# Selective scan in a two-layer vision kernel: tiles of four states by 32 channels instead of two states by 64

## The chip, the cores and the metric

The kernel runs on one core of one Trainium2 chip. The metric is the device time of one execution in microseconds (us). Before the change it was 23158.47 us, the median of three runs (23155.23 to 23162.02).

## The reference

Two residual layers act on `x` of shape (8, 64, 64, 192); each is fed the group-normed input. Layer 0 is a Mamba-2 block with convolutions and an MLP; the change leaves its work alone. Layer 1 is a four-direction selective scan (SS2D), per image of 4096 pixels:

```python
xz = einsum('bhwc,dc->bhwd', x, in_proj_w); xc, z = split(xz)          # 384 channels each
xc = silu(depthwise_conv3x3(xc) + conv_b)
xs = [xc by rows, xc by columns, and both reversed]                     # K = 4 sweeps
dts, B, C = split(einsum('bkdl,kcd->bkcl', xs, x_proj_weight))          # 12 + 16 + 16 rows
delta = softplus(einsum('bkrl,kdr->bkdl', dts, dt_projs_weight) + bias)
A = -exp(A_logs)                                                        # (4, 384, 16 states)
# for every pixel, in order:
h = exp(delta * A) * h + (delta * u) * B                                # per channel and state
y = sum over states of h * C
out = (layernorm(sum of the four sweeps' y + xs * Ds) * silu(z)) @ out_proj_w.T
```

So every sweep of every image runs 384 x 16 recurrences over 4096 pixels, in float32.

## The kernel before, in words

Layer 1 works image by image (8 images). For each image a planner (`Flow`) interleaves three things in one stretch: `finish` of the image before (layer norm, gate, output projection), `front` of this one (projection, 3x3 convolution, copies of the result in DRAM: `xo[0]` by rows, `xo[1]` by columns, `xo[2]` by tokens) and the `prologue` of its scan. The planner orders each engine's instructions by weights written beside each step. Then `main()` runs the scan, whose instructions stay in the order in which the code issues them, engine by engine.

The scan of an image has 32 *steps*: 4 sweeps of 8 chunks of 512 pixels (`TT`). A step has 24 *units*: here 8 pairs of states `p` (in the order of `ORDER`) by 3 channel blocks `d` of 128 channels. I number the units of a step q = 0 to 23. A tile of a unit has 128 partitions, two states by 64 channels, and two halves `f` of 512 pixels, for two groups of 64 channels. One turn of the loop in `main()` for unit u issues, in this order:

- `load_c` (at d = 0): C rows of a later pair, repeated over 64 partitions, into `cb` (3 buffers).
- `run(u)`: two scan instructions on VectorE (DVE), one per half: `hs` from the decays `ea`, the inputs `g` in PSUM and the carried state `cy` (L1662); then on GpSimd (POOL) the copy of the last column into `cy` (L1674) and the multiplication by `cb` (L1676).
- `decay(u + 2)`: two exponentials on ScalarE (ACT) into `ea` (L1620), which has 3 buffers: the tile of unit u + 2 is that of unit u - 1.
- two or three `weigh`: ACT multiplies the turned product delta*u of one 128-pixel block by one state's B (L1605), into `pw` (8 buffers). Of 16 states x 4 blocks a step weighs 56; the list `todo` runs 2 instructions past what the next pair needs (10 are made ahead, a pair needs 8 or 6).
- `supply(u + 1)`: TensorE (PE) transposes the blocks of `pw` into `g` (L1646), 4 buffers of one half. For 4 of 32 pair-blocks (`on_diagonal`) it multiplies delta*u by a diagonal matrix of B instead (`dg`, L1634), with no `weigh`.
- `collect(u - 2)`: PE sums over the two states with `sel`, one matmul of 64 output partitions per half, side by side (L1691); in sweep 0 the skip term is added there (L1689). `add(u - 3)`: DVE adds a finished `y` to `yacc`.
- pieces of `prepare(s + 1)`, the next step's inputs, placed at fixed q: loads (q 0), `project` (2 to 4), `keep` (5: `xdbl`), `turn_b` and `keep_b` (6, 7), then for three blocks `step` (PE, `p_dt`), `soft` (ACT exp and ln, `spa`; at q 8, 10, 13), `delta` (DVE, `de`), `turn` and `keep_du` (`duT`), and `repeat_delta`, which copies delta over the partitions (`dr`).

A float32 matmul stands in the profile as two MATMUL records, a transpose as one. All DMAs are issued by SP in one queue, which waits in order.

Of the kernel before, what the change touches and what calls it, by code (L numbers as in the profile page):

```python
# [16 lines left out]
CP, CT = 96, 2  # L17
# [12 lines left out]
NP1 = N // 2  # L30
ND = 8
ORDER = [0, 4, 1, 5, 2, 6, 3, 7]
# [1001 lines left out]
def layer1(tc, consts, x1s, mv1, out, w_in, w_x, w_dt, w_out):  # L1034
# [7 lines left out]
    with ExitStack() as ctx:  # L1042
# [9 lines left out]
        wi = wp.tile([CP, CT, 2 * DIN], F32, name="wi1")  # L1052
# [7 lines left out]
        an = wp.tile([128, K, NP1, 2 * DT], F32, name="an")  # L1060
# [6 lines left out]
        sel = wp.tile([128, 64], F32, name="sel")  # L1067
        for i in range(2):
            nc.vector.tensor_copy(sel[i * 64 : i * 64 + 64], ident[i * 64 : i * 64 + 64, i * 64 : i * 64 + 64])
# [24 lines left out]
        zero = yacc[:, 0, : ND * 128].rearrange("p (n b) -> p n b", b=128)  # L1094
        nc.gpsimd.memset(zero, 0.0)
        dzs = [dgp.tile([ND, 128 * 128], F32, name=f"dz{i}") for i in range(2)]
        for t in dzs:
            nc.sync.dma_start(out=t.rearrange("n (a b) -> a n b", b=128), in_=zero)

        def scaled(w, b, half):  # L1100

            for ct in range(CT):
                r = yield step(
                    "ACT",
                    0.6,
                    lambda: [
                        nc.scalar.activation(
                            w[:, ct],
                            wi[:, ct, half * DIN : half * DIN + DIN],
                            AF.Copy,  # L1110
                            scale=sc[:, b * CT + ct : b * CT + ct + 1],
                        )
                    ],
                )
            return r
# [326 lines left out]
        def scan(xo):  # L1442
# [11 lines left out]
            units = [(s, p, d) for s in range(len(steps)) for p in ORDER for d in range(DT)]  # L1454
# [3 lines left out]
            def first(s):  # L1458
                return steps[s][1] == (0 if steps[s][0] < 2 else NS1 - 1)

            def prepare(s, bank=lambda name: mp.tile([128, TT], F32, name=name, tag="mm")):
# [5 lines left out]
                def load():  # L1467
                    st["xc"] = pools["pr1"].tile([128, DT, TT], F32, name="xc")
                    o(nc.sync.dma_start(out=st["xc"], in_=xo[k % 2][:, :, c * TT : c * TT + TT]))
                    st["ut"] = pools["pr1"].tile([128, NB1, DIN], F32, name="ut", bufs=1)  # L1470
                    if k % 2 == 0:
                        src = xo[2][c * TT : c * TT + TT].rearrange("(j p) m -> p j m", p=128)
                        o(nc.sync.dma_start(out=st["ut"], in_=src))
                    else:
                        for i in range(2):
                            src = xo[2].rearrange("(h w) m -> w h m", w=WI)[c * RT + i : c * RT + RT : 2]
                            o(nc.sync.dma_start(out=st["ut"][i * 64 : i * 64 + 64], in_=src.rearrange("j h m -> h j m")))
# [21 lines left out]
                def spread():  # L1499
                    dz = dzs[s % 2]  # L1500
                    st["dg"] = dg = pools["dg1"].tile([128, ND, 128], F32, name="dg")
                    o(nc.sync.dma_start(out=dz[:, :: 128 + 1], in_=xds[s % 2][N - ND : N, 0:128]))
                    o(nc.sync.dma_start(out=dg, in_=dz.rearrange("n (a b) -> a n b", b=128)))
# [11 lines left out]
                def keep_b():  # L1515
                    st["bt"] = bt = pools["pr1"].tile([128, NB1, N], F32, name="bt")
                    o(nc.vector.tensor_copy(bt.rearrange("p a b -> p (a b)"), st["p_b"][:, : NB1 * N]))
                    st["duT"] = pools["pr1"].tile([128, NB1, DIN], F32, name="duT")
# [31 lines left out]
                def keep_du(d):  # L1550
# [4 lines left out]
                            st["ut"][:, :, d * 128 : d * 128 + 128],  # L1555
# [12 lines left out]
                    9: [(delta, 0), (step, 1)],  # L1568
                    10: [(soft, 1)],
                    11: [(delta, 1), (turn, 0), (repeat_delta, s, 0)],  # L1570
                    12: [(keep_du, 0), (step, 2)],
                    13: [(soft, 2)],
                    14: [(delta, 2), (turn, 1)],
                    15: [(keep_du, 1)],
                    16: [(turn, 2)],
                    17: [(keep_du, 2)],
                    20: [(repeat_delta, s, 1)],
                    21: [(repeat_delta, s, 2)],
                }

            def repeat_delta(s, d):

                state[s]["dr", d] = dr = pools["dr1"].tile([128, 2, TT], F32, name="dr")
                de = state[s]["de", d]
                for f in range(2):
                    for i in range(2):
                        o(nc.sync.dma_start(out=dr[i * 64 : i * 64 + 64, f], in_=de[f * 64 : f * 64 + 64]))

            def load_c(s, p):
                state[s]["cb", p] = cb = pools["bc1"].tile([128, TT], F32, name="cb")  # L1590
                for i in range(2):
                    o(
                        nc.sync.dma_start(
                            out=cb[i * 64 : i * 64 + 64], in_=state[s]["cd"][2 * p + i].partition_broadcast(64)
                        )
                    )

            def weigh(s, p, j, i):

                st = state[s]  # L1600
                if i == 0:
                    st["pw", p, j] = pools["pw1"].tile([128, 2 * DT, 2, 64], F32, name="pw")
                n = 2 * p + i
# [3 lines left out]
                        st["duT"][:, j].rearrange("p (g c) -> p g c", c=64),  # L1607
# [5 lines left out]
            def decay(u):  # L1613
                s, p, d = units[u]
                k, c = steps[s]
                made["e", u] = ea = pools["e1"].tile([128, 2, TT], F32, name="ea")
                for f in range(2):
                    at = 2 * d + f
                    o(
                        nc.scalar.activation(  # L1620
                            ea[:, f], state[s]["dr", d][:, f], AF.Exp, scale=an[:, k, p, at : at + 1]
# [3 lines left out]
            def supply(u):  # L1625
                s, p, d = units[u]
                gs = [pools["g1"].tile([128, TT], F32, name="g") for f in range(2)]
                made["g", u, 0], made["g", u, 1] = gs
                for j in range(NB1):
                    if on_diagonal(p, j):  # L1630
# [302 lines left out]
```

## Time and profile before

| what | value |
|---|---|
| median of three runs | 23158.47 us |
| the profiled execution's own time | 23175.73 us |
| its span, first to last instruction | 23174.0 us |
| busy: PE, DVE, ACT, POOL | 94%, 91%, 87%, 70% |
| granted TensorE clock | 0.971 of full speed |
| DMA, one queue | 1976 MB, 31.9% of 16 engines |
| first scan instruction of image 1, its last | 7302.3 us, 9333.4 us: 2031.1 us for 32 steps |
| from there to the first scan of image 2 | 252.4 us |

"Busy" is the share of the span in which an engine had at least one instruction in flight; matmul ends are modelled, so a busy PE can have room left. Waits name what came last before an engine went on. Layer 0 takes the first fifth of the span; the eight scans follow, with a shorter stretch of front and finish between them.

### The profile page before, as it was taken

The numbers are of one execution on the slowest core, as the hardware profiler recorded it, in microseconds if no ns is written. First come the engines' busy times: TensorE is split into PE (matmuls) and PEld (weight loads), VectorE is DVE, ScalarE is ACT, GpSimd is POOL, SyncE is SP. The second block draws the span as 40 slices with busy tenths as digits, with TensorE's granted clock in tenths as the row PEclk, the third lists the DMA queues.
The fourth block names the chain that finished last, engine by engine and source line by source line (L and its number), as shares of the span: only waits on it lengthen the run. The fifth ranks groups of instructions, "written<-read, shape, count | busy, mean of one in ns | idle before, by whom it ended". The sixth has DMA issues, their size and how long they took to land.

```text
span 23174.0 us, 348545 instructions
## 1 busy us (share of the span) xinstructions
PE 21762.7 (94%) x118788; PEld 11070.5 (48%) x118788; DVE 21110.3 (91%) x22093; ACT 20048.9 (87%) x35418; POOL 16109.5 (70%) x12872
## 2 busy tenths in 40 slices
PE   8999999979998999899999999999999999999999
PEld 4444444435554555455545544554455445544554
DVE  7888888869998999899989998999899989998998
ACT  5666666759997999799979997999899989988998
POOL 1111111139995999599959995999599869976997
PEclk8999999989999999999999999999999999999999
DMA  1111111133333333333333334333433343333332
GB/s 52 45 44 41 45 45 45 42 96 92 95 93 111 92 92 94 111 94 93 90 114 93 92 87 117 95 92 88 117 92 92 89 117 93 93 91 113 92 94 75
DMA packets 1738653, 1998.38 MB, mean 86 GB/s; under 512 B 537280, under 2 KB 1034848, under 8 KB 1727648
## 3 DMA queue, kind: packets, MB, share of 16 engines
q1 hardware_dynamic: 1736864, 1976.07, 31.9%
q8 instruction: 934, 15.30, 0.3%
q14 instruction: 855, 7.00, 0.1%
HBM read 1360.20 MB, written 212.60 MB: 68 GB/s over the span
## 4 chain that ended last, share of the span: by engine, by line
PE 48%; ACT 22%; DVE 11%; POOL 8%; issue 6%; DMA 3%; SPq 2%; DVEq 0%; POOLq 0%; ACTq 0%
PE g L1646 10%; PE y L1691 10%; ACT ea L1620 10%; ACT pw L1605 9%; POOL hs L1676 7%; DVE hs L1662 3%; PE g L1634 3%; PE p_f L957 3%; DVE xs L1209 3%; PE p_d L1488 2%; PE p_x L450 2%; PE p_f L977 2%; PE p_dt L1523 2%; DMA dr<-de 2%; PE p_o L874 2%
## 5 line engine op out<-in xcount | busy, mean ns | idle before, releaser
L1676 POOL TENSOR_TENSOR hs<-hs,cb 128x1024 f32<-128x1024 f32 x6144 | 14584.3, 2374 | 496.4 <-POOL cy L1674 4.2
L1662 DVE TENSOR_TENSOR_SCAN hs<-ea,cy,g 128x512 f32<-128x512 f32 x10752 | 12894.9, 1258 | 187.2 <-PE g L1646 178.1
L1620 ACT ACTIVATE ea<-dr,an 128x512 f32<-128x512 f32 x12288 | 8139.8, 710 | 528.5 <-DVE hs L1662 507.0
L1605 ACT ACTIVATE pw<-duT,bt 128x384 f32<-128x384 f32 x14336 | 7832.7, 600 | 23.5 <-DVE duT L1552 23.5
L1691 PE MATMUL y<-hs,sel 128*64 128x512 f32 x24576 | 6635.2, 618 | 360.0 <-POOL hs L1676 338.6
L1646 PE MATMUL g<-ident,pw 128*128 128x128 f32 x43008 | 6089.9, 281 | 41.1 <-ACT pw L1605 4.8
L1646 PEld LDWEIGHTS g<-ident,pw 128*128 128x128 f32 x43008 | 4612.5, 141 | 2522.6 <-issue 1254.9
L1674 POOL COPY cy<-hs 128x2 f32<-128x2 f32 x6144 | 1160.7, 189 | 2262.0 <-DVE hs L1662 2228.8
L1634 PEld LDWEIGHTS g<-dg,duT 128*64 128x64 f32 x24576 | 1557.4, 136 | 2053.0 <-issue 1484.6
L1634 PE MATMUL g<-dg,duT 128*64 128x128 f32 x24576 | 2257.9, 282 | 169.4 <-DVE hs L1662 106.1
L1691 PEld LDWEIGHTS y<-hs,sel 128*64 128x64 f32 x24576 | 1234.2, 135 | 1563.0 <-issue 865.6
L1662 DVE TENSOR_TENSOR_SCAN hs<-ea,g 128x512 f32<-128x512 f32 x1536 | 1751.8, 1197 | 129.1 <-PE g L1646 116.8
L367 POOL TENSOR_TENSOR s<-xs 96x512 f32<-96x512 f32 x64 | 121.7, 1902 | 2139.6 <-DVE xs L345 1850.2
L1523 PE MATMUL p_dt<-xdbl,wd 13*128 13x512 f32 x1536 | 857.5, 639 | 96.2 <-DVE duT L1552 71.0
L1209 DVE SCALAR_TENSOR_TENSOR xs<-pad,p,xs 128x4096 f32<-128x4096 f32 x192 | 860.9, 4484 | 50.7 <-ACT xs L1199 43.5
L367 POOL TENSOR_TENSOR s<-sq 96x512 f32<-96x512 f32 x128 | 180.1, 1407 | 942.7 <-ACT sq L380 864.4
L1488 PE MATMUL p_d<-xc,wx 128*44 128x512 f32 x1536 | 788.6, 596 | 19.9 <-DMA xc<-xo 19.9
L957 PE MATMUL p_f<-h,wf 96*128 96x512 f32 x1536 | 762.4, 635 | 44.1 <-ACT zs L552 27.5
L345 DVE SCALAR_TENSOR_TENSOR x<-xx,p,x 96x512 f32<-96x512 f32 x1024 | 784.8, 816 | 15.2 <-ACT x L334 15.0
L345 DVE SCALAR_TENSOR_TENSOR xs<-xin,p,xs 96x512 f32<-96x512 f32 x1024 | 746.1, 768 | 3.6 <-ACT xs L334 3.6
L977 PE MATMUL p_f<-m,wf 128*96 128x512 f32 x1536 | 696.1, 604 | 0.0
L1545 PEld LDWEIGHTS p_du<-ident,de 128*128 128x128 f32 x3072 | 323.9, 141 | 610.1 <-DVE de L1536 406.3
(205 smaller groups left out, 19972.1 us busy)
## 6 DMA issues: line engine op xcount, KB each, us to landing
cb<-cd SPq DMA_DIRECT2D x4096, 128.0 KB
dr<-de SPq DMA_DIRECT2D x3072, 128.0 KB
xc<-xo SPq DMA_DIRECT2D x256, 768.0 KB
dg<-dz SPq DMA_DIRECT2D x256, 512.0 KB
e<-csd SPq DMA_DIRECT2D x256, 384.0 KB
xl<-x SPq DMA_DIRECT2D x256, 384.0 KB
ut<-xo SPq DMA_DIRECT2D x128, 768.0 KB
ut<-xo SPq DMA_DIRECT2D x256, 384.0 KB
```

The lines of the kernel that those rows point to most:

```text
L345: nc.vector.scalar_tensor_tensor(im(out[:, ct]), tap(ct, j), w[:, ct, j : j + 1], im(out[:, ct]), ALU.mult, ALU.add)
L957: nc.tensor.matmul(ps, wf1[:, ct, mt * 128 : mt * 128 + 128], h[:, ct], start=ct == 0, stop=ct == 1)
L1209: nc.vector.scalar_tensor_tensor(xs, tap(j), kw[:, d, j : j + 1], xs, ALU.mult, ALU.add)
L1488: nc.tensor.matmul(st["p_d"][:44], wx[:, d, k], st["xc"][:, d], start=d == 0, stop=d == DT - 1)
L1523: nc.tensor.matmul(ps, st["wd"][32:45, d * 128 : d * 128 + 128], xds[s % 2][32:45], start=True, stop=True)
L1605: nc.scalar.activation(st["pw", p, j][:, :, i], st["duT"][:, j].rearrange("p (g c) -> p g c", c=64), AF.Copy, scale=st["bt"][:, j, n : n + 1],
L1620: nc.scalar.activation(ea[:, f], state[s]["dr", d][:, f], AF.Exp, scale=an[:, k, p, at : at + 1])
L1634: nc.tensor.matmul(gs[f][i * 64 : i * 64 + 64, j * 128 : j * 128 + 128], state[s]["duT"][:, j, (2 * d + f) * 64 : (2 * d + f) * 64 + 64], ...
L1646: nc.tensor.transpose(gs[f][:, j * 128 : j * 128 + 128], state[s]["pw", p, j][:, 2 * d + f].rearrange("p a b -> p (a b)"), ident,)
L1662: nc.vector.tensor_tensor_scan(rev(h[:, f]), rev(ea[:, f]), rev(g[f]), 0.0 if first(s) else state[s - 1]["cy"][:, p, d, f : f + 1], ALU.mu ...
L1676: o(nc.gpsimd.tensor_mul(h, h, bc(st["cb", p], 1, [128, 2, TT])))
L1691: o(nc.tensor.matmul(y[half[f]], sel, hc[:, f], start=p == ORDER[0] and k > 0, stop=p == ORDER[-1]))
```

## The change

A tile of a unit is now four states by 32 channels. There are 4 quadruples `p` (`NQ1`) by 6 groups `g` of 64 channels (`NG`), again 24 units of the same tile size, in plain order. What follows from it and what comes along:

- `collect` works at every second unit and sums over four states with four matmuls of 32 output partitions, side by side.
- `on_diagonal` is true for block 0 of every quadruple and also for block 1 of the odd ones: 6 of 16. There `supply` issues four matmuls of 32 columns per half and block; `weigh` falls from 56 to 40 per step. The `pw` tiles lie in two pools, 3 buffers for even and 2 for odd quadruples; 12 `weigh` are made ahead, which is what the first quadruple needs. The counts per turn are 1, 1, 2, 2, 1, 1 in even and 1, 2, 3, 2, 2, 2 in odd quadruples.
- delta goes to DRAM (`store_delta`) and is read back 12 times per step, repeated over four states; `dr` has 8 buffers instead of 4.
- the diagonals go to two DRAM tiles in three DMAs, and are read per quadruple by `load_c`; in the prologue `spread` stands ahead of the scan.
- `cb` has 2 buffers, four DMAs each; `xc` is loaded a step earlier by `load_x` (q 10); `duT` takes the load that `ut` had, and is multiplied in place.
- the input projection's weights are loaded by DMA for each image and scaled in place.

```diff
-ORDER = [0, 4, 1, 5, 2, 6, 3, 7]
+NQ1 = N // 4
+NG = DIN // 64
...
-        for i in range(2):
-            nc.vector.tensor_copy(sel[i * 64 : i * 64 + 64], ident[i * 64 : i * 64 + 64, i * 64 : i * 64 + 64])
+        for i in range(4):
+            nc.vector.tensor_copy(sel[i * 32 : i * 32 + 32], ident[i * 32 : i * 32 + 32, i * 32 : i * 32 + 32])
...
         def scaled(w, b, half):
+            src = w_in.rearrange("(t p) m -> p t m", p=CP)[:, :, half * DIN : half * DIN + DIN]
+            r = yield step("SP", 0.1, lambda: [nc.sync.dma_start(out=w, in_=src)])
...
-            units = [(s, p, d) for s in range(len(steps)) for p in ORDER for d in range(DT)]
+            units = [(s, p, g) for s in range(len(steps)) for p in range(NQ1) for g in range(NG)]
...
+            def load_x(s):
+                if s < len(steps):
+                    k, c = steps[s]
+                    state[s]["xc"] = xc = pools["pr1"].tile([128, DT, TT], F32, name="xc")
+                    o(nc.sync.dma_start(out=xc, in_=xo[k % 2][:, :, c * TT : c * TT + TT]))
...
-                    9: [(delta, 0), (step, 1)],
-                    10: [(soft, 1)],
-                    11: [(delta, 1), (turn, 0), (repeat_delta, s, 0)],
+                    9: [(delta, 0), (store_delta, s, 0), (step, 1)],
+                    10: [(soft, 1), (load_x, s + 1)],
+                    11: [(delta, 1), (store_delta, s, 1), (turn, 0)],
                     12: [(keep_du, 0), (step, 2)],
-                    13: [(soft, 2)],
-                    14: [(delta, 2), (turn, 1)],
-                    15: [(keep_du, 1)],
+                    13: [(soft, 2), (repeat_delta, s, 0)],
+                    14: [(delta, 2), (store_delta, s, 2), (turn, 1)],
+                    15: [(keep_du, 1), (repeat_delta, s, 1)],
                     16: [(turn, 2)],
-                    17: [(keep_du, 2)],
-                    20: [(repeat_delta, s, 1)],
-                    21: [(repeat_delta, s, 2)],
+                    17: [(keep_du, 2), (repeat_delta, s, 2)],
+                    18: [(repeat_delta, s, 3)],
+                    20: [(repeat_delta, s, 4)],
+                    21: [(repeat_delta, s, 5)],
...
+            def store_delta(s, d):
+                state[s]["dd", d] = dd = dp.tile([128, TT], F32, name=f"dd{d}", bufs=2)
+                o(nc.sync.dma_start(out=dd, in_=state[s]["de", d]))
+
+            def repeat_delta(s, g):
+                n = (s * NG + g) % 8
+                state[s]["dr", g] = dr = pools["dr0" if n < 6 else "dr1"].tile([128, 2, TT], F32, name="dr")
                 for f in range(2):
-                    for i in range(2):
-                        o(nc.sync.dma_start(out=dr[i * 64 : i * 64 + 64, f], in_=de[f * 64 : f * 64 + 64]))
+                    at = (2 * (g % 2) + f) * 32
+                    rows = state[s]["dd", g // 2][at : at + 32]
+                    o(nc.sync.dma_start(out=dr[:, f], in_=rows.partition_broadcast(4)))
...
+                for i in range(4):
+                    o(nc.sync.dma_start(out=cb[i * 32 : i * 32 + 32], in_=st["cd"][4 * p + i].partition_broadcast(32)))
+                for j in range(p % 2 + 1):
+                    st["dg", p, j] = dg = pools["dg1"].tile([128, 4, 128], F32, name="dg")
+                    src = dzs[s % 2][j][4 * p : 4 * p + 4].rearrange("n (a b) -> a n b", b=128)
+                    o(nc.sync.dma_start(out=dg, in_=src))
...
-                    st["pw", p, j] = pools["pw1"].tile([128, 2 * DT, 2, 64], F32, name="pw")
-                n = 2 * p + i
+                    st["pw", p, j] = pools[f"pw{p % 2}"].tile([128, 2 * NG, 4, 32], F32, name="pw")
+                n = 4 * p + i
...
-                                        gs[f][i * 64 : i * 64 + 64, j * 128 : j * 128 + 128],
-                                        state[s]["duT"][:, j, (2 * d + f) * 64 : (2 * d + f) * 64 + 64],
-                                        state[s]["dg"][:, 2 * p + i - (N - ND)],
+                                        gs[f][i * 32 : i * 32 + 32, j * 128 : j * 128 + 128],
+                                        st["duT"][:, j, at : at + 32],
+                                        st["dg", p, j][:, i],
                                         start=True,
                                         stop=True,
+                                        tile_position=(0, i * 32),
...
+                if g % 2 == 0:
+                    return
+                hc = [made.pop(("hc", u - 1)), made.pop(("hc", u))]
+                for i in range(4):
+                    o(
+                        nc.tensor.matmul(
+                            y[i * 32 : i * 32 + 32],
+                            sel,
+                            hc[i // 2][:, i % 2],
+                            start=p == 0 and k > 0,
+                            stop=p == NQ1 - 1,
+                            tile_position=(0, i * 32),
+                        )
+                    )
...
             def on_diagonal(p, j):
-                return j == 0 and 2 * p >= N - ND
+                return j <= p % 2
...
-                for name, n in (("pr1", 2), ("dr1", 4), ("pw1", 8), ("bc1", 3), ("e1", 3)):
+                for name, n in (("pr1", 2), ("dr0", 6), ("pw0", 3), ("bc1", 2), ("e1", 3), ("dg1", 3)):
...
-                for t in todo[:10]:
+                for t in todo[:12]:
                     yield step("ACT", 0.55, lambda: weigh(*t), f.free["ACT"])
...
-                ready["spread"]()
                 supply(0)
...
-                    for _ in range(((2, 2, 2) if on_diagonal(p, 0) else (3, 3, 2))[d]):
+                    for _ in range(((1, 1, 2, 2, 1, 1), (1, 2, 3, 2, 2, 2))[p % 2][g]):
                         if t := next(rest, None):
                             weigh(*t)
```

## The prediction, made before the changed kernel ran

> **What bounds the kernel now.** I read the page's parts 1 and 5, then busy time in a window inside one scan, then the timeline of ACT and DVE for one step.
>
> ```profile
> PE 21762.7 (94%) x118788; PEld 11070.5 (48%) x118788; DVE 21110.3 (91%) x22093; ACT 20048.9 (87%) x35418; POOL 16109.5 (70%) x12872
> L1676 POOL TENSOR_TENSOR hs<-hs,cb 128x1024 f32<-128x1024 f32 x6144 | 14584.3, 2374 | 496.4 <-POOL cy L1674 4.2
> L1662 DVE TENSOR_TENSOR_SCAN hs<-ea,cy,g 128x512 f32<-128x512 f32 x10752 | 12894.9, 1258 | 187.2 <-PE g L1646 178.1
> L1605 ACT ACTIVATE pw<-duT,bt 128x384 f32<-128x384 f32 x14336 | 7832.7, 600 | 23.5 <-DVE duT L1552 23.5
> ...
> 6000.00:6500.00 500.00, 482.64 (x3095) 252.51 (x3093) 495.52 (x471) 491.50 (x878) 480.47 (x385) 1.00 0.35 94
> ```
>
> The last line gives PE, PEld, DVE, ACT, POOL in 500 us of a scan, at full clock: DVE is busy 99.1%. A third of PE's or ACT's work could go and DVE, whose work the change leaves, would still need its time. POOL needs 24 x (2.374 + 0.189) = 61.5 us a step, close behind.
>
> ```profile
> 10322.46 1.32 ACT L1620 ACTIVATE ea<-dr,an 128x512 f32<-128x512 f32 x2
> 10323.69 1.11 ACT L1605 ACTIVATE pw<-duT,bt 128x384 f32<-128x384 f32 x2
> 10324.70 0.58 ACT L1530 ACTIVATE spa<-p_dt 128x512 f32<-128x512 f32 x1
> 10325.31 0.63 ACT L1531 ACTIVATE spa<-spa 128x512 f32<-128x512 f32 x1
> 10325.84 1.32 ACT L1620 ACTIVATE ea<-dr,an 128x512 f32<-128x512 f32 x2
> ...
> 10328.08 1.32 ACT L1620 ACTIVATE ea<-dr,an 128x512 f32<-128x512 f32 x2
> ...
> 10331.47 1.32 ACT L1620 ACTIVATE ea<-dr,an 128x512 f32<-128x512 f32 x2
> ...
> 10322.04 4.89 DVE L1662 TENSOR_TENSOR_SCAN hs<-ea,cy,g 128x512 f32<-128x512 f32 x4
> 10326.84 0.66 DVE L1536 SCALAR_TENSOR_TENSOR de<-spa,p_dt 128x512 f32<-128x512 f32 x1
> 10327.42 2.44 DVE L1662 TENSOR_TENSOR_SCAN hs<-ea,cy,g 128x512 f32<-128x512 f32 x2
> 10330.21 2.45 DVE L1662 TENSOR_TENSOR_SCAN hs<-ea,cy,g 128x512 f32<-128x512 f32 x2 [0.34 <-PE g L1646]
> 10332.58 0.66 DVE L1536 SCALAR_TENSOR_TENSOR de<-spa,p_dt 128x512 f32<-128x512 f32 x1
> ```
>
> These are units q 8 to 11 of a step. Pitches, start to start: a unit's two scans 2.34 us (2.46 with `keep_b`), a DVE piece 0.58; on ACT 1.23 for two exponentials, 0.506 per `weigh`, 1.14 for a `soft`. A step without a wait is 24 x 2.35 + 10 x 0.58 + 0.12 = 62.3 us. Copies into `xdbl` start at 10316.64 and 10379.54 in sweep 1 (62.9 us a step, as in sweeps 2 and 3) and at 9674.38 and 9739.56 in sweep 0 (65.18). So DVE waits 0.6 us a step in sweeps 1 to 3 (at q 8 and 10, for PE behind `p_dt`) and 2.9 in sweep 0, where PE has the skip matmuls too.
>
> **How late ACT runs.** `decay(u+2)` cannot start before scan u-1 ends (three `ea` buffers). Call its delay behind that the lag: next lag = lag + ACT's work in the turn - DVE's pitch one turn earlier, at least 0.03. Above: q 8 starts 0.45 after the scans of q 7 end at 10322.01; then 0.45 + 2.24 + 1.14 - 2.47 = 1.36 (seen 10325.84 - 10324.47 = 1.37), 1.37 + 2.24 - 2.45 = 1.16 (1.15), 1.15 + 3.38 - 2.93 = 1.60 (1.61). The recurrence holds to 0.02 us, and costs nothing before, since `weigh` runs ahead of need.
>
> **The change, part by part.**
>
> *DVE, POOL*: same instructions, tiles and counts. Zero.
>
> *ACT*: 16 fewer `weigh` a step, 8.1 us less. But `weigh` is now exactly as far ahead as the next quadruple, so the last of a turn's `weigh` at q 11 and q 23 gates the scan after it. With counts 1, 2, 3, 2, 2, 2 and `soft` at q 8 and 10: lag at q 8 is 0.03; q 9: 0.03 + 1.23 + 1.52 + 1.14 - 2.46 = 1.46; q 10: 1.46 + 2.24 - 2.34 = 1.36; q 11: 1.36 + 3.38 - 2.95 = 1.79. There two exponentials and two `weigh` take 2.33 to the last output, then the transpose (0.28) and hand-overs, estimated 0.16: the scan of q 12 can start 4.56 after scan 10 ends. Its turn would be 2.95 - 0.08 = 2.87 (`delta` hides part). Wait: 1.7 us. At q 23 the lag is 0.2, the wait 0.1. At q 5 and q 17 one `weigh` is due; no wait. `weigh` in runs of 32 elements instead of 64 I take at the old 0.506, since elements per partition are equal; bounds 0.39 (the mean of ACT's 128x128 row, L654) and 0.60 (no overlap of one `weigh` with the next). Nine lie between q 8 and q 11, so the wait has 0.7 to 2.5 us.
>
> *PE*: per step 120 transposes for 168 (0.109 pitch), the sums at half of 1.07 a unit, and 576 records L1634 instead of 96.
>
> ```profile
> 10007.67 0.66 PE L1634 MATMUL g<-dg,duT 128*64 128x128 f32 x8
> 10008.26 0.88 PE L1646 MATMUL g<-ident,pw 128*128 128x128 f32 x6
> 10009.06 1.08 PE L1691 MATMUL y<-hs,sel 128*64 128x512 f32 x4
> ```
>
> Eight L1634 take 0.59 to the next group: two side by side per 0.109, and 0.15 for the start and the change of tile width. No row has four side by side. Bounds: four in the time of two (0.109), or no faster per matmul (0.0545). At the first an even unit needs 16/4 x 0.109 + 0.15 + 6 x 0.109 + 0.09 + 0.54 = 1.87 us, an odd one 0.87 + 0.15 + 0.53 + 0.54 = 2.1, and the step's pieces 8.0 (L1488 2.9, `p_b` 0.4, `p_dt` 3.2, `p_du` 1.5): 55.6 of 62.3, covered by DVE. I take it, as the pair's second member starts 6 ns after the first. The remaining PE delay behind `p_dt` (0.3 to 0.5 at q 8 and 10) falls under ACT's 1.7. In sweep 0, counted from the start of scan 2, POOL frees the sums of unit 1 at 4.0; then PE has 3.1 (skip, sums, `p_d`), 2.3, 3.65, 1.95 and 4.7 for the turns q 3 to 7 and 1.4 to the first half of unit 9: 21.1, where DVE alone would be at 17.7. With ACT's rest DVE waits 3.8 us by q 12 (from ACT's 1.8 alone to 5 with another skip matmul late) instead of 2.9.
>
> The Trainium skill ("TensorE: Matmul & The Clock Gate", section "Wait — 56ns, not 53.3ns?") speaks against this: starts never closer than about 25 ns on average, and about 62 ns per matmul where the sequencer decodes in software. By 62 an odd unit's 32 records alone would be an estimated 2.0 us instead of 0.87, and the time about 26,200 us. No row here decides it; the pairs show 54 ns per matmul at their best.
>
> *DMA on SP*: 43 issues a step instead of 33, some 0.57 each, so 25 us of 62. `load_c` waits for `cb` (two buffers: POOL 2.7 to 4.3 behind the scan), then four issues, then `dg`; behind it stand `repeat_delta` and loads due 6 or more turns later. `dg` is asked for at 4.3 + 4 x 0.57 + 2 x 0.39 = 7.4 us of a quadruple and lands some 3 us later (an estimate, from 4.75 for twice the bytes, below); `supply` needs it after five scans, at 12.5. `dr` through DRAM is asked for 6 to 9 turns (15 us) ahead. Zero, with 2 us to spare for `dg`.
>
> *First step of an image*: it takes 71.0, because SP reads the diagonals only after the last store:
>
> ```profile
> 9590.41 4.75 DMA dg<-dz
> ```
>
> DVE stands 3.64 and 0.94 us for it. With `spread` in the prologue this goes: -4.6.
>
> *Between scans* (252.4 us, eight times): two more `weigh` on ACT ahead of the last gates (+1.0); the second weight scaling behind `ysq`, which moves `p_x` from 9348.42 to about 9350 (+1.7). The weights' DMA lies beside 10 us in which ACT idles; the trip of delta beside 12 `weigh`, 6.1 us. I take +3, bounds -4 and +10.
>
> **Sum.** Sweeps 1 to 3: +1.7 + 0.1 - 0.6 = 1.2 a step, 23 steps (the last prepares nothing): 28. Sweep 0: 7 x 0.9 = 6. First step: 0.9 - 4.6 = -3.7. Between: +3. Per image 33, times 8: 267 us. The profiled execution took 23175.73 us (span 23174.0), so 23,443; the median lies 17 below it: 23,430 us, 1.2% slower.
>
> **Rivals.**
>
> 1. *PE becomes the bound.* Four narrow matmuls go no faster per record than two: an odd unit 1.74 + 0.15 + 0.53 + 0.54 = 2.96, an even one 2.3; 12 x 5.26 + 8 = 71.1 a step, +8.2 x 248: 25,200 us. If the sums gain nothing either, 0.54 x 24 more a step: 28,400. For it: no row with four; against: 6 ns between pair members.
> 2. *Faster.* ACT's wait at q 12 does not form, because the narrow `weigh` is cheap or PE's delays at q 8 and 10 go without it. Then 62.4 a step: -0.5 x 184, sweep 0 with 1.5 of waits instead of 2.9: -80, first steps -37, between +24: 22,970 us. It decides below 0.7 us of wait per step. For it: PE and ACT both lose work; against: the recurrence fits the trace.
> 3. *SP's queue is late.* `dg` of an odd quadruple lands after q 5 or 17, because two loads follow four `cb` issues behind POOL. 2 us late twice a step, +4 x 256 on top of the forecast: 24,450. Against: the 2 us to spare.
> 4. *No change that counts.* Waits gone and waits added balance within 0.2% (about what a measurement of this kernel can tell from no change).
>
> **Chances.** The forecast 0.46, rival 1 0.24, rival 3 0.06, rival 2 0.15, rival 4 0.09. Faster 0.15, same 0.09, slower 0.76. The range reaches down to a faster case that keeps half of the gain, 23,090, and up to rival 1 with the sums side by side, 25,200; beyond lie about 0.08 and 0.1. The forecast's own range is 23,250 to 23,650.
>
> **What would show it.** Right: DVE still 97% busy in the scan, one wait per step of 1 to 2.6 us at the unit after q 11, put down to PE g, and behind it ACT pw; ACT near 90%, PE near 90%. First step about 66 us. Rival 1: DVE under 90%, waiting for PE at every odd quadruple, L1634 pitch near 54 ns. Rival 3: PE waits for DMA dg. Rival 2: no wait of over 0.5 us in a step, and 62.4 us between `xdbl` copies. Wrong above all would be the price of four matmuls side by side, which no row shows.

## The result and the profile after

The changed kernel takes 24865.97 us (median of 4 runs, 24858.28 to 24868.12), the kernel before in the same series 23160.25 (4 runs, 23155.23 to 23162.76): ratio 1.0736, 95% interval 1.0718 to 1.0755. It is 7.4% slower; I had forecast slower by 1.2%. The profiled execution took 24858.28 us. Parts 1 and 5 of its page (busy time, share and count of each engine; then groups of instructions with busy time, mean ns of one, idle time ahead and what ended most of it):

```profile
PE 21486.9 (86%) x228996; PEld 11562.5 (47%) x228996; DVE 21275.3 (86%) x22095; ACT 18250.8 (73%) x31319; POOL 16181.0 (65%) x12872
L1691 POOL TENSOR_TENSOR hs<-hs,cb 128x1024 f32<-128x1024 f32 x6144 | 14577.5, 2373 | 498.1 <-POOL cy L1689 7.5
L1677 DVE TENSOR_TENSOR_SCAN hs<-ea,cy,g 128x512 f32<-128x512 f32 x10752 | 12975.2, 1262 | 1315.7 <-PE g L1661 1082.8
L1617 ACT ACTIVATE pw<-duT,bt 128x384 f32<-128x384 f32 x10240 | 5757.7, 600 | 46.6 <-DVE duT L1557 46.6
```

DVE and POOL do the same work in the same time as before (the scan instruction 1262 ns for 1258), and ACT and PE do less. What grew is the idle time ahead of the scan, from 187.2 to 1315.7 us for this group. The window of 500 us inside a scan that the prediction used (PE, PEld, DVE, ACT, POOL, then granted clock, share of the DMA engines, GB/s):

```profile
6000.00:6500.00 500.00, 430.04 (x6000) 244.78 (x6004) 456.51 (x430) 396.29 (x682) 440.13 (x349) 0.96 0.40 121
```

DVE, 99.1% busy there before, is 91.3% busy, and no other engine is above it: nothing has become the bound, the engines wait in turns. The waits of the whole span say for what (engine and what it makes, what it waits for, us in all, times, longest):

```profile
PE g L1661 <- ACT pw L1617: 1391.7, 964, 7.1
ACT ea L1632 <- DMA dr<-dd: 1058.0, 615, 7.6
PE g L1648 <- DMA dg<-dz: 317.5, 349, 4.1
```

The prediction had the first in kind; the second is new: the exponentials wait for delta, which the prediction had put at zero. A step from its timeline (start, duration, engine, line, tiles, count, idle time ahead and its releaser):

```profile
9051.88 9.70 SPq L1598 DMA_DIRECT2D dr<-dd  x5
...
9068.50 0.72 ACT L1632 ACTIVATE ea<-dr,an 128x512 f32<-128x512 f32 x1 [2.58 <-DMA dr<-dd]
9069.13 1.10 ACT L1617 ACTIVATE pw<-duT,bt 128x384 f32<-128x384 f32 x2
9071.51 0.72 ACT L1632 ACTIVATE ea<-dr,an 128x512 f32<-128x512 f32 x1 [1.27 <-DMA dr<-dd]
9074.38 0.72 ACT L1632 ACTIVATE ea<-dr,an 128x512 f32<-128x512 f32 x1 [2.15 <-DMA dr<-dd]
...
9076.00 2.26 PE L1648 MATMUL g<-dg,duT 128*32 128x128 f32 x32 [2.84 <-DMA dg<-dz]
...
9085.60 1.08 PE L1648 MATMUL g<-dg,duT 128*32 128x128 f32 x32
...
9075.13 1.28 DVE L1677 TENSOR_TENSOR_SCAN hs<-ea,cy,g 128x512 f32<-128x512 f32 x1 [1.17 <-ACT ea L1632]
9080.20 2.45 DVE L1677 TENSOR_TENSOR_SCAN hs<-ea,cy,g 128x512 f32<-128x512 f32 x2 [3.22 <-PE g L1661]
9084.85 2.45 DVE L1677 TENSOR_TENSOR_SCAN hs<-ea,cy,g 128x512 f32<-128x512 f32 x2 [2.19 <-PE g L1661]
```

The step begins at 9059.77. Its last reads of `dr`, asked for up to 9061.6, reach ACT one by one, the last at 9074.4. The exponentials hold up the `weigh` behind them in ACT's order, those the transposes, those the scans: DVE stands 6.6 us here. SP took 9.7 us to issue five reads, and what stands behind them on its queue, `cb` and `dg`, is late as well: PE waits 2.84 us for `dg`, and after that idle time it runs at half clock (32 MATMUL records take 2.26 us, and 1.08 ten microseconds later).

The transfer itself, 9060 to 9070 in 40 slices (busy share of the 16 DMA engines in tenths, and GB/s):

```profile
DMA  2222222222222222222647463484499843332245
GB/s 106 90 98 98 98 98 98 98 98 98 98 98 98 98 98 98 98 98 98 238 148 229 131 213 98 172 260 115 137 295 317 223 94 111 117 109 82 106 131 190
```

For 4.5 us hardly anything runs but these reads, at a flat 98 GB/s and a quarter of the DMA engines, though several are in flight. One read is 256 KB, so 2.7 us; twelve a step are 32 us of 69. Other transfers reach 317 GB/s a moment later.

Where the 1,683 us between the two profiled executions lie, by the times of the first and last scan instruction of each image: 1,424 us in the eight scans (2208.4 us each instead of 2030.3) and 260 us in the seven stretches between them (289.7 instead of 252.6).

### The profile page after: what moved, and what is told of

It reads as the page before. It is cut to its first block, busy times and chain, and to the rows that moved or that the text cites. A ratio compares the mean times of both kernels' runs of the same rounds, so it can differ in the third digit from the quotient of the medians.

```text
span 24856.6 us, 569276 instructions
## 1 busy us (share of the span) xinstructions
PE 21486.9 (86%) x228996; PEld 11562.5 (47%) x228996; DVE 21275.3 (86%) x22095; ACT 18250.8 (73%) x31319; POOL 16181.0 (65%) x12872
## 5 line engine op out<-in xcount | busy, mean ns | idle before, releaser
L1677 DVE TENSOR_TENSOR_SCAN hs<-ea,cy,g 128x512 f32<-128x512 f32 x10752 | 12975.2, 1262 | 1315.7 <-PE g L1661 1082.8
L1648 PE MATMUL g<-dg,duT 128*32 128x128 f32 x147456 | 5681.1, 283 | 787.0 <-DVE hs L1677 419.1
L1661 PE MATMUL g<-ident,pw 128*128 128x128 f32 x30720 | 5127.2, 294 | 1392.9 <-ACT pw L1617 1391.7
L1648 PEld LDWEIGHTS g<-dg,duT 128*32 128x32 f32 x147456 | 3931.0, 112 | 4143.6 <-issue 2420.7
L1617 ACT ACTIVATE pw<-duT,bt 128x384 f32<-128x384 f32 x10240 | 5757.7, 600 | 46.6 <-DVE duT L1557 46.6
L1661 PEld LDWEIGHTS g<-ident,pw 128*128 128x128 f32 x30720 | 3393.7, 145 | 2884.6 <-ACT pw L1617 1659.1
L1708 PE MATMUL y<-hs,sel 128*32 128x512 f32 x24576 | 3560.2, 649 | 34.8 <-POOL hs L1691 34.2
L1708 PEld LDWEIGHTS y<-hs,sel 128*32 128x32 f32 x24576 | 498.3, 110 | 745.2 <-issue 578.8
L1550 PE MATMUL p_du<-ident,de 128*128 128x128 f32 x3072 | 533.3, 301 | 160.2 <-DVE de L1541 160.1
```

What stands on the lines that cost most here:

```text
L1617: nc.scalar.activation(st["pw", p, j][:, :, i], st["duT"][:, j].rearrange("p (g c) -> p g c", c=32), AF.Copy, scale=st["bt"][:, j, n : n + 1],
L1648: nc.tensor.matmul(gs[f][i * 32 : i * 32 + 32, j * 128 : j * 128 + 128], st["duT"][:, j, at : at + 32], st["dg", p, j][:, i], start=True, ...
L1661: nc.tensor.transpose(gs[f][:, j * 128 : j * 128 + 128], st["pw", p, j][:, 2 * g + f].rearrange("p a b -> p (a b)"), ident,)
L1677: nc.vector.tensor_tensor_scan(rev(h[:, f]), rev(ea[:, f]), rev(gs[f]), 0.0 if first(s) else state[s - 1]["cy"][:, p, g, f : f + 1], ALU.mult,
L1708: nc.tensor.matmul(y[i * 32 : i * 32 + 32], sel, hc[i // 2][:, i % 2], start=p == 0 and k > 0, stop=p == NQ1 - 1, tile_position=(0, i * 32),)
```

## The experiments

All times below are medians, each ratio against the kernel before on the same chip: 23167.33 us beside the first four versions, 23165.49 beside the next three.

**Delta read from SBUF instead of DRAM.** This takes away both the trip through DRAM and the narrow read, and adds issues on SP.

```diff
-                    rows = state[s]["dd", g // 2][at : at + 32]
-                    o(nc.sync.dma_start(out=dr[:, f], in_=rows.partition_broadcast(4)))
+                    rows = state[s]["de", g // 2][at : at + 32]
+                    for i in range(4):
+                        o(nc.sync.dma_start(out=dr[i * 32 : i * 32 + 32, f], in_=rows))
```

`store_delta` does nothing here.

> The changed kernel, but delta is repeated straight from its SBUF tile: four DMAs of 32 partitions for each half of a group, 48 a step, and no store to DRAM. Theory A (the repeated read from DRAM runs on about four of the sixteen DMA engines: 48 packets of 2 KB per us at 87 ns each, so 2.7 us for each of 12 reads a step, and the decay tiles come late): the wait of 2.1 us at q 5, those at q 0 and q 6 and most of the 38 us between scans go; a step takes 64 us, some 253 us lie between scans, 23,350 to 23,550 us in all. Theory B (the trip through DRAM and its waits, whatever number of engines reads): the same here. Theory C (the other new DMAs, the diagonals above all, or SP's queue are what makes DVE wait; SP would issue 76 a step here): it stays above 24,300 us.

Measured: 24186.17 us, ratio 1.0437 (1.0423 to 1.0451). 680 us come back, less than theories A and B expected and more than C: a step of sweeps 1 to 3 takes 66.4 us for 68.7, and 276.5 us lie between two scans, not 253. ACT still waits 414.4 us for `dr` in all. A read from SBUF also costs SP more than one from DRAM: in this version SP issues them 0.63 us apart, in the next one 0.46 (medians).

**The DRAM trip kept, each read split in four.** The same last two lines, with `rows` still from `dd`.

> The changed kernel with the trip of delta through DRAM kept, but each repeated read split in four reads of 32 rows, one for each state, as from SBUF. Theory A: the reads spread over all engines, a step takes 64 to 64.5 us, 255 to 275 us lie between scans (the wait for the store stays there), 23,400 to 23,700 us. Theory B: no better than the changed kernel by more than 200 us, 24,600 us or more.

Measured: 23964.63 us, ratio 1.0342 (1.0328 to 1.0356). 901 us come back, more than without the trip, though less than theory A expected (a step of sweeps 1 to 3 takes 65.6 us, not 64 to 64.5). So it is not the trip through DRAM, and not the number of issues (48 reads a step instead of 12), but the form of the read. ACT's wait for `dr` falls from 1058.0 us to

```profile
ACT ea L1633 <- DMA dr<-dd: 66.4, 40, 5.6
```

What is left stands at the unit after q 11, as the prediction had it, and at the one behind that, which it had not. This kernel's timeline, units q 9 to 13 of a step:

```profile
8890.20 2.45 DVE L1678 TENSOR_TENSOR_SCAN hs<-ea,cy,g 128x512 f32<-128x512 f32 x2 [0.35 <-PE g L1662]
...
8895.93 2.45 DVE L1678 TENSOR_TENSOR_SCAN hs<-ea,cy,g 128x512 f32<-128x512 f32 x2 [0.33 <-PE g L1662]
8898.30 0.66 DVE L1541 SCALAR_TENSOR_TENSOR de<-spa,p_dt 128x512 f32<-128x512 f32 x1
8899.73 2.45 DVE L1678 TENSOR_TENSOR_SCAN hs<-ea,cy,g 128x512 f32<-128x512 f32 x2 [0.78 <-issue]
8902.16 0.69 DVE L1557 TENSOR_TENSOR duT<-p_du,duT 128x512 f32<-128x512 f32 x1
8904.11 1.28 DVE L1678 TENSOR_TENSOR_SCAN hs<-ea,cy,g 128x512 f32<-128x512 f32 x1 [1.25 <-ACT pw L1618]
...
8890.22 1.08 PE L1649 MATMUL g<-dg,duT 128*32 128x128 f32 x32
8891.23 0.66 PE L1662 MATMUL g<-ident,pw 128*128 128x128 f32 x4
...
8895.94 0.65 PE L1649 MATMUL g<-dg,duT 128*32 128x128 f32 x16
8896.51 0.44 PE L1662 MATMUL g<-ident,pw 128*128 128x128 f32 x2
8899.31 0.66 PE L1662 MATMUL g<-ident,pw 128*128 128x128 f32 x4 [2.36 <-ACT pw L1618]
...
8902.05 1.08 PE L1649 MATMUL g<-dg,duT 128*32 128x128 f32 x16
8903.07 1.37 PE L1662 MATMUL g<-ident,pw 128*128 128x128 f32 x6
```

The two small waits for PE are those behind `p_dt`, which were there before. The 0.78 us are for the last `weigh`, through the transposes at 8899.31. The 1.25 us bear the name of `pw`, but the last `weigh` ahead of it had ended by 8901.0, and it is PE that is late: after its own wait of 2.36 us the granted clock is 0.66 of full speed from 8900 to 8905 (1.00 in the 5 us before and after), and 16 records that took 0.57 us to the next group at 8895.94 take 1.02 at 8902.05.

That is no single case. Of the 184 steps of sweeps 1 to 3 that prepare a next one, 80 have a mean clock below 0.75 through q 12 and take 4.57 us for it; the others take 3.00. At q 0, 114 of them take 3.72 us, the others 2.94. In the kernel before no step has a lowered clock there, and these units take 2.93 and 2.91. So the half clock behind PE's waits is worth an estimated 1.2 us a step (0.68 at q 12, 0.48 at q 0, from these means).

**The narrow read alone, in the kernel before.** A source repeated twice instead of four times, six reads a step:

```diff
-                    for i in range(2):
-                        o(nc.sync.dma_start(out=dr[i * 64 : i * 64 + 64, f], in_=de[f * 64 : f * 64 + 64]))
+                    o(nc.sync.dma_start(out=dr[:, f], in_=dd[f * 64 : f * 64 + 64].partition_broadcast(2)))
```

> The kernel before with one part of the change alone: delta is stored to DRAM and read back repeated over its two states, one read of 128 partitions per half, six a step. Theory A, with as many engines as there are repeats: 64 packets of 87 ns on each of two engines, 5.6 us a read and 33 us a step, the reads of blocks 1 and 2 (asked for at q 20 and 21, the last needed at q 0) land 6 to 15 us late: 24,600 to 27,000 us, packets of 2 KB at about 2 of 16 engines while they run. Theory B, or engines shared out in another way: the trip of 3 us or so hides behind the turns ahead of it, 23,160 to 23,450 us.

Measured: 28532.94 us, two runs, ratio 1.2314 (1.2292 to 1.2337). That is beyond the range expected for the narrow read, on its side. The transfers of the kernel, 6137 to 6147, and what ACT waits for:

```profile
GB/s 344 328 377 266 307 291 197 162 166 109 170 115 193 152 223 207 223 223 178 147 100 72 164 231 184 164 270 131 74 25 41 33 41 49 49 49 49 49 33 49
```

```profile
ACT ea L1620 <- DMA dr<-dd: 5124.7, 956, 10.0
```

A read repeated twice runs at a flat 49 GB/s, half of the fourfold one: 24.5 GB/s per repetition in both. Those are 48 and 24 packets of 2 KB per us, some 85 ns each, so about four and two at a time. That fits a number of DMA engines that follows the outermost dimension of the access pattern, which a leading repetition makes 4 or 2. Here six reads need 5.3 us each, 32 us of a step as in the changed kernel, but this kernel asks for two of its three blocks only at q 20 and 21 of a step, just ahead of their use: ACT stands up to 10 us for one, and a step takes 84 us.

**`weigh` earlier, with delta from SBUF.** The first version with one line changed:

```diff
-                    for _ in range(((1, 1, 2, 2, 1, 1), (1, 2, 3, 2, 2, 2))[p % 2][g]):
+                    for _ in range(((1, 1, 2, 2, 1, 1), (3, 3, 3, 2, 1, 0))[p % 2][g]):
```

> As x1, and the counts of weigh in odd quadruples 3, 3, 3, 2, 1, 0 instead of 1, 2, 3, 2, 2, 2, so that the last block of the next quadruple is ready a turn or more ahead. The theory of ACT's lag: the wait at q 12 (1.7 us by the forecast's recurrence) goes, a step takes 62.4 to 62.9 us; 290 to 400 us less than x1, 23,000 to 23,150 us, as fast as the kernel before or 0.5% faster. Rival, that PE holds the same units up: at most 100 us less than x1.

Measured: 24230.79 us, ratio 1.0454 (1.044 to 1.0469): no gain. The waits at q 11, 12, 23 and 0 are gone (mean pitches 2.93, 2.93, 2.36 and 2.92 for 3.63, 3.80, 2.65 and 3.40), but q 5, 6, 13 and 14 have grown by 2.5 us (4.77, 3.10, 2.76, 3.29 for 3.52, 2.51, 2.45, 2.93). At q 5 and 6 what SP brings comes late, and later than in the first version: ACT waits 719.3 us for `dr` in all (414.4 there) and PE 554.4 us for `dg` (250.7). At q 13 and 14 PE runs at a mean clock below 0.75 in 53 and 112 of 184 steps, which take 3.20 and 3.52 us there; the others take 2.58 and 2.93. That the exponentials wait longer because more `weigh` stands in their way is likely, but not shown. One cause of lateness hid the other, so the question had to be asked again on the version whose reads arrive in time:

**`weigh` earlier, with the wide reads from DRAM.** The same line in the second version.

> The changed kernel with each repeated read of delta split in four reads of 32 rows, and the multiplications by delta of odd quadruples made in counts 3, 3, 3, 2, 1, 0 after its six units instead of 1, 2, 3, 2, 2, 2. Theory (what is left after the narrow reads is the last multiplications, which stand behind ACT's backlog): the waits at q 11, 12, 23 and 0 go (they cost 1.3 and 0.8 us a step), and the waits at q 8 and 10 for PE behind the delta projection stay: 24,000 less 250 x 2.1 is some 23,440 us, between 23,400 and 23,650. Rival (ACT is simply too late in this phase, so that earlier multiplications make the decays late instead, as they did with delta read from SBUF): no gain, 23,900 to 24,000.

Measured: 23504.63 us, ratio 1.0149 (1.0135 to 1.0163), 460 us less than without it, and the middle of the range. A step of sweeps 1 to 3 falls from 65.59 to 63.53 us. In the step shown DVE runs without a gap from q 12 on; what remains is PE behind `p_dt`. In the mean q 13 and 14 still take 0.26 and 0.34 us more than before the change, at q 14 by the clock again (88 of 184 steps below 0.75 take 3.60 us, the others 2.92):

```profile
8885.76 2.45 DVE L1678 TENSOR_TENSOR_SCAN hs<-ea,cy,g 128x512 f32<-128x512 f32 x2 [0.33 <-PE g L1662]
...
8899.99 4.79 DVE L1678 TENSOR_TENSOR_SCAN hs<-ea,cy,g 128x512 f32<-128x512 f32 x4
8904.69 0.67 DVE L1557 TENSOR_TENSOR duT<-p_du,duT 128x512 f32<-128x512 f32 x1
8905.28 11.81 DVE L1678 TENSOR_TENSOR_SCAN hs<-ea,cy,g 128x512 f32<-128x512 f32 x10
```

**The kernel before with two `weigh` fewer in hand.**

```diff
-                for t in todo[:10]:
+                for t in todo[:8]:
...
-                rest = iter(todo[10:])
+                rest = iter(todo[8:])
```

> The kernel before with the first 8 multiplications by delta made ahead of the first scan of an image instead of 10, and so with two fewer in hand through all steps; nothing else. The recurrence of ACT's lag in the prediction, with this kernel's 10 instructions a quadruple of units, gives waits of 1.25 us at q 12, 0.15 at another unit and 0.73 at the step's end, 2.1 us a step: 400 to 600 us more, 23,550 to 23,750. Rival (the lead of the multiplications is not what matters, PE's own work is): under 100 us more.

Measured: 23704.07 us, ratio 1.0238 (1.0224 to 1.0252), 539 us more. Two instructions of ACT, moved behind the need and not added, cost 2.4%: a step of sweeps 1 to 3 grows by 2.33 us (recurrence: 2.1), most of it at q 8, 11, 13 and 23. The recurrence has the sum and the step's end (0.78 us at q 23, 0.73 expected); of its 1.25 at q 12 there are 0.41 at q 11, and it had none of the 0.57 at q 8. In its groups the idle time of PE ahead of the transposes is nearly all for `pw`; it had been 41.1 us in all before:

```profile
L1646 PE MATMUL g<-ident,pw 128*128 128x128 f32 x43008 | 6262.3, 282 | 1147.9 <-ACT pw L1605 1143.6
```

So the lead in `weigh`, which the prediction's recurrence turns on, is what matters in the kernel before too, although ACT has the same work.

**The weights' DMA alone, in the kernel before.** `scaled` as in the change, nothing else.

> The kernel before with only one part of the change: the input weights of a half are loaded by DMA for each image and scaled in place, instead of scaled from a copy kept in SBUF. Theory (this is a small part of the 25 us that each stretch between two scans has gained): 2 to 4 us in each of the stretches, 15 to 30 us more in all. Rival (it is the main part of those 25 us): 100 us or more. If the load is hidden: within 10 us of before.

Measured: 23260.99 us, ratio 1.0044 (1.003 to 1.0058), 95 us more, far above the 15 to 30 expected and just under the rival's 100: each stretch between scans takes 265.2 us instead of 252.6, and the scans stay at 2030.0. A table of the times from the end of an image's last scan, in us, mean of the seven stretches, shows where:

| event between two scans | before | weights' DMA alone | wide reads (2nd version) | changed kernel |
|---|---|---|---|---|
| last copy `xt` starts | 173.8 | 182.8 | 182.8 | 182.7 |
| first `spa` | 217.9 | 228.9 | 229.3 | 229.7 |
| first `weigh` | 226.5 | 239.5 | 239.3 | 239.5 |
| first exponential `ea` | 231.6 | 244.6 | 248.8 | 251.4 |
| fourth exponential `ea` | 233.4 | 246.4 | 254.4 | 259.5 |
| last gated `yacc` | 238.5 | 251.5 | 259.4 | 264.6 |
| first scan of the next image | 252.6 | 265.2 | 277.2 | 289.7 |

Down to the first `weigh` the changed kernel is as late as the one with the weights' DMA alone: 13 us of the 37. ACT waits 6.03 us for the weights in the stretch after image 1, but the first copy into the padded image starts only 0.4 us later for it (17.4 us after the last scan, 16.9 before); the 9 us up to `xt` come after that, in a part where the planner has put the instructions in another order. Which of its choices costs them I have not separated. Below that line it is delta again: the fourth exponential comes later by 8 us more with wide reads and by 13 as changed, and the gate's table load and `z` stand behind it on ACT. With wide reads the DRAM trip is the smaller part of this. The first version, which has no trip, has its fourth exponential at 252.0 and the next image's first scan at 276.5, close to the second's 254.4 and 277.2. It has 48 reads as well, for which SP takes 30.34 us after image 1 (12 took 7.55 us in the kernel with the weights' DMA alone), and its first exponentials stand 2.1 to 2.6 us apart, about four issues each. The last 11 us, of the changed kernel:

```profile
9998.27 2.12 SPq L1589 DMA_DIRECT2D dd<-de  x1
10009.75 2.53 SPq L1598 DMA_DIRECT2D dr<-dd  x4
10012.38 1.62 SPq L1589 DMA_DIRECT2D dd<-de  x1
10023.70 2.38 SPq L1598 DMA_DIRECT2D dr<-dd  x4
10026.18 3.28 SPq L1427 DMA_DIRECT2D out_x<-xl  x3
...
10001.21 0.72 ACT L1632 ACTIVATE ea<-dr,an 128x512 f32<-128x512 f32 x1 [5.84 <-DMA dr<-dd]
10003.90 0.72 ACT L1632 ACTIVATE ea<-dr,an 128x512 f32<-128x512 f32 x1 [1.96 <-DMA dr<-dd]
...
10039.14 11.22 DVE L1677 TENSOR_TENSOR_SCAN hs<-ea,g 128x512 f32<-128x512 f32 x10 [12.00 <-DMA out_x<-xl]
```

SP issues a store of delta, the four reads of it 11.4 us later, then the next store, and behind all of them the output's stores, for which DVE waits 12 us: it was ready for the scan at 10027.1. The exponentials 2.67 us apart are the narrow reads arriving. The 11.4 us are about four reads of 2.7. They hang on the form of the reads: in the second version, where only that differs, SP issues the reads 2.1 us after such a store (9773.02 to 9775.17, and 9782.53 to 9784.65). That the store stands behind the narrow reads on the engines they share would explain it, and was not tried by itself.

**The diagonals' copy ahead of the scan, in the kernel before.**

```diff
                 def spread():
...
-                    o(nc.sync.dma_start(out=dz[:, :: 128 + 1], in_=xds[s % 2][N - ND : N, 0:128]))
+                    if s:
+                        fill()
...
                 r = yield step("DVE", 0.7, ready["keep"])
+                yield step("SP", 0.1, fill0, r)
```

`fill` and `fill0` hold the line that is taken out, for the later steps and for the first.

> The kernel before with one thing taken from the change: the copy of an image's first eight rows of B into the diagonals in DRAM is asked for in the stretch ahead of the scan, behind the copy into xdbl, not at the scan's start; reading them back stays at the scan's start. Theory (the prediction's term for the first step: DVE stands 3.6 and 0.9 us there for these diagonals, and nothing else is late): the first step takes 66 to 67.5 us instead of 71, so 28 to 40 us less in all, 23,120 to 23,140, and this version is faster than both kernels by about the least that can be told. Rival (the first step of the changed kernel was shorter because its sums and transposes need less of PE): no change in the first step, within 10 us of before.

Measured: 23158.38 us, median of 11 runs, against 23166.91 of 15: ratio 0.9997, 0.9988 to 1.0006. The first step is shorter as expected, 66.9 us for 70.7 (mean of images 1 to 7), and with it the scan (2027.0 for 2030.3); each stretch between scans takes 0.7 us more. In all that is 22 us of the profile, 0.1%, less than the 28 to 40 expected, and no difference that the times can tell. The step of the prediction is right, its rival is not; it is only small.

## Why the prediction was right or wrong

The direction was right and the size was not: +267 us forecast, +1,683 measured in the profiled executions. By its steps:

1. *"`dr` through DRAM is asked for 6 to 9 turns (15 us) ahead. Zero"*: **this step failed**, and it holds the largest part. The reads were costed by when they are asked for, not by how long they take. The one row of the profile before that I used for a DMA's length was `dg`; none had a source repeated four times. Twelve reads of 2.7 us on a quarter of the engines are 32 us of a step, asked for in the last 11 turns and one behind the other, so in the step shown the last one is used 13 us after SP had issued it. Widening the reads alone gives 901 us back. The Trainium skill ("DMA: Bandwidth & Descriptors", section "Rules for kernel authors") says it outright: the outermost dimension sets the number of engines, and a leading repetition of c copies keeps the transfer on at most c of them. The runs agree, with 98 GB/s at four and 49 at two, and it was there to be read beside the diff's `partition_broadcast(4)`.

2. *ACT's lag*: right in mechanism; **the clock behind the wait was missing**. Once the reads are wide the lag at q 9 is 1.48 us, where the recurrence gave 1.46. At q 10 and 11 it is 0.83 and 1.29 instead of 1.36 and 1.79, because DVE's waits for PE (point 3) lengthen its pitch; with them put in, the recurrence gives 0.85 and 1.28. The wait after q 11 is then 0.86 us. What it has no term for is 0.76 at q 12, nearly all of it the half clock that PE has after its wait for the last `weigh`, and 0.11 at q 13. At the step's end it gave 0.1, and q 23 and q 0 show 0.8 together, 0.48 of it the clock again. Together that is 1.6 us a step, some 290 us in 184 steps. It goes, with the 0.86, when `weigh` comes earlier (460 us, 2.06 a step), and the kernel before gains the same kind of wait when its lead is taken (539 us).

3. *"The remaining PE delay behind `p_dt` (0.3 to 0.5 at q 8 and 10) falls under ACT's 1.7"*: right in the sum. The waits stay, 0.53 us at q 8 and 0.43 at q 10 in the second version (0.25 and 0.46 before), but they let ACT catch up: with the 0.86 after q 11 they make 1.82, for 1.7 forecast. In sweep 0, where 0.9 us a step were forecast, the second version gains 1.5 (66.7 for 65.2) and the changed kernel 5.2.

4. *PE, four matmuls side by side*: right. 32 records take 1.01 us to the next group (8890.22 to 8891.23 in the second version); 8 passes of 0.109 and 0.15 make 1.02. The first rival, in which they go no faster than two, is out: PE's busy time fell, and no wait in the steps has its place. The 62 ns per matmul that the prediction weighed against this (the Trainium skill, "TensorE: Matmul & The Clock Gate", section "Wait — 56ns, not 53.3ns?") did not show here: it is 32 ns for one, the change of tile included; the 25 ns of the same section are not undercut.

5. *SP, "2 us to spare for `dg`"*: it holds in the second version, whose waits name no `dg` for PE. With narrow reads SP is itself held up, and PE waits 317.5 us for `dg` in all; with 48 reads from SBUF a step it waits 250.7. So the third rival came true in part, through the reads of delta.

6. *First step of an image −4.6*: 65.65 us in the changed kernel for 70.7 (images 1 to 7), −5.0, and −3.9 for the diagonals alone.

7. *Between scans +3, bounds −4 and +10*: failed, +37. About 13 come with the weights' DMA, where +1.7 had been put on the scaling's place and nothing on what the planner would make of the rest; the others are delta's way into `dr`, which was taken to lie "beside 12 `weigh`, 6.1 us". With wide reads that way is longer than the `weigh` by 8 us, most of it without the DRAM trip too; with narrow ones it is longer by 13, and 11 more come of the output's stores behind it on SP.

In sum: by the medians 901 us for the narrow reads and 460 for the last `weigh` of odd quadruples; by the profiled executions some 90 for the weights' DMA, 82 for the rest between scans, and 146 in the scans that are left over, mostly at q 8, 13 and 14. The half clock is spread over these terms: in the changed kernel the steps with a mean clock below 0.75 at q 0 and q 12 (103 and 95 of 184) take 0.84 and 1.47 us longer there than the others, an estimated 1.2 of the 6.0 us that a step of sweeps 1 to 3 has gained. Rivals 2 and 4, faster or equal, needed the waits for `weigh` not to form, and they formed. None of the versions that keep the new tiles beats the kernel before, and the diagonals' copy, moved over alone, changes nothing that can be told. That 24,866 us lies inside the stated range is luck: the range reached up to 25,200 for PE as the bound, which it did not become. Left open: what in the planner's order makes the 9 us ahead of `xt`.

## What to carry to other kernels

Cost a DMA by its shape as well as by its bytes and by when it is asked for: here a source repeated four times in its outermost dimension ran on a quarter of the engines, and several such reads shared the same ones. When producers are moved "just in time", work out how late their engine already is at the place where the last one is due; two instructions of lead were worth 2.4% here. Count a wait of TensorE for what follows it as well: 2.4 us of waiting were followed by 3.4 us at half clock. And when two causes of lateness lie on one path, taking away the smaller one first can show nothing.

## What the runs showed of the hardware

Reads repeated four and two times ran at 98 and 49 GB/s. With the same bytes in reads of 32 rows the traffic of a step goes up to 361 (6100 to 6163 of the version with wide reads and earlier `weigh`, in 40 slices):

```profile
GB/s 0 21 4 13 1 63 127 144 169 185 311 17 166 0 131 191 287 177 160 191 142 144 142 86 142 154 240 130 82 130 155 113 152 125 126 177 218 361 98 0
```

SP, which issued four narrow reads in 2.53 us at 10009.75, took 9.70 us for five of them at 9051.88. The waits of its queue in that stretch (9050 to 9063) are put down to earlier reads and to ACT, which still held the buffers:

```profile
SPq L1598 <- DMA dr<-dd: 4.4, 2, 2.7
SPq L1598 <- ACT ea L1632: 2.2, 2, 1.9
```

Here a slow transfer also held up the queue behind it. And TensorE pays for the stall after it is over, as in the second version above: the granted clock (the column behind the five engines' busy times) of the changed kernel falls to half behind the 2.84 us of waiting for `dg`, and is full again some ten microseconds later, though PE is busy for most of them:

```profile
9068.00:9072.00 4.00, 4.00 (x40) 1.90 (x38) 4.00 (x5) 2.23 (x4) 3.84 (x5) 1.00 0.46 143
9072.00:9076.00 4.00, 1.16 (x4) 0.19 (x3) 2.83 (x3) 1.85 (x4) 3.77 (x3) 0.92 0.77 229
9076.00:9080.00 4.00, 2.95 (x35) 1.76 (x36) 0.98 (x2) 4.00 (x8) 2.55 (x2) 0.50 0.32 38
9080.00:9084.00 4.00, 4.00 (x43) 1.86 (x41) 2.45 (x2) 2.61 (x6) 1.20 (x2) 0.50 0.25 30
9084.00:9088.00 4.00, 4.00 (x56) 2.60 (x52) 3.15 (x4) 1.70 (x5) 1.90 (x3) 0.80 0.37 107
9088.00:9092.00 4.00, 4.00 (x75) 2.48 (x72) 2.94 (x3) 3.97 (x9) 3.92 (x3) 1.00 0.00 0
```
